# Two-layer convolution block: sampling weights laid out with the eight ky of a cell side by side, layer-norm sums moved from GpSimd to VectorE, and a kernel table built from 16 steps

## The chip, the core and the metric

The kernel runs on one core of a Trainium2 chip. The metric is the device time of one execution in microseconds (us). Three runs of the kernel before took 12570.41, 12572.89 and 12574.23 us, so the median is 12572.89 us. The profile below is of a further execution.

Engine names in the profile: PE is TensorE's matmul, PEld its weight load, DVE is VectorE, ACT ScalarE, POOL GpSimd, SP the engine that issues most DMAs.

## What is computed

The input `x` is 32 images of 128 channels, 32 by 32 pixels, all in float32. Two layers follow, each added to its input after a group norm.

```python
# layer 0: a state-space convolution along the 1024 positions, a gate, a layer norm
h  = einsum('bdl,de->ble', u, W_enc) + b_enc            # 128 -> 1024
K  = 2 * einsum('dn,dnl->dl', Cc * Bd, exp(dtA * t)).real   # t = 0..63
y  = gelu(causal_conv(h, K) + D * h)
g  = y @ W_glu; g = g[..., :1024] * sigmoid(g[..., 1024:])
out = layernorm(h + g) @ W_dec + b_dec
# layer 1: a depthwise 8x8 convolution whose 64 taps sample at learned places
off = depthwise_conv3x3(x)                              # dx, dy of each tap and pixel
for tap in 64:                                          # bilinear sample, times a weight
    acc += bilinear(x, px + off_x, py + off_y) * weight[tap]
out = gelu(batchnorm(acc))
```

## The kernel before

There are three stages. `ssm_kernel_table` (lines 42 to 159) builds K for all 1024 channels: it evaluates exp and sine/cosine at 32 (channel group, mode) pairs times 64 steps, so its VectorE operations have 2048 elements per partition.

`ssm_convolution` (186 to 371) runs over eight groups of 128 channels. `encode(k)` projects the 32 images (line 237) and VectorE copies the sums out of PSUM (L242). Only for k = 0 it also makes the group norm of each image, in five steps that a hand-written loop (264 to 284) puts out for three images in turn: a row sum on ACT (L169), a matmul over groups (L172), the mean and the squares on ACT (L174, L175), a second matmul (L178), and root, reciprocal and scaling (L180 to L182). The normalised image is stored to memory as `u_d` by a DMA that ACT's queue issues (L267). `convolve` then multiplies by a table of K (L320).

`main_block` (590 to 1348) is the long stage. It interleaves two streams of work by `run_along` (577), which always lets the stream with the smaller share of its planned cost speak next. The order of instructions on every engine is therefore fixed when the program is built, and no measured time enters it.

- The first stream is the rest of layer 0, on tiles of 512 positions, two for each image and eight output chunks m for each tile. A chunk has eight matmuls for the gate (L815), eight for the value (L838), one for h (L854), one to decode (L743). ACT takes the sigmoid (L822), VectorE makes the product (L846) and `r = h + g` (L867), ACT squares r (L875). Layer norm needs the sum over chunks of r and of its square: `add_up` (735 to 739) adds them up on GpSimd in two halves of 256, called at L745 for r and at L876 for the square.
- The second stream is layer 1 of an image some way behind. An image has 17 packs, each of m = 8 to 16 slots (12 packs have 16); a slot is one pairing of a source column with a tap column. Per slot the tile `ds` holds 160 cells, eight tap rows ky times 20 rows v, as weights over 128 partitions: two sides of 64 partitions, of eight window columns times eight window rows. ACT makes hat functions of the distance in y in the tile `dhy` (L1153, L1154), and VectorE multiplies `ds`, the hats in x that a DMA brings from memory, by them (L1159, in four parts for a pack). TensorE multiplies by the image's windows `dxw` (L1235). A pack has four pieces, and a piece has a PSUM bank for each side; four banks are there (`psam`, line 627), so a piece can start when the piece two before it has been read out. VectorE does that, scaling with the tap weights into `prod` (L1251), and GpSimd sums over ky (L1278) and adds up to the image (L1286).

Pieces 1 to 3 are each a block of eight ky by four v in two matmuls of two v each. Piece 0 has five small blocks: 2 ky by 6 v, 2 by 4, 2 by 2, 3 by 1 and 4 by 1. Every float32 matmul in the code is two matmul records in the profile, and the two sides run as neighbours on different halves of the array. Before the change a slot's cells lie as 20 v for each ky, so a matmul of pieces 1 to 3 reads its moving operand as runs of two neighbouring floats:

```python
to = t[:, lo:hi].rearrange("p (s k v) -> p s k v", s=m, k=rows)
...
ap=[frm.ap[0], [CELLS, m], [step * NV + skew, rows], [1, r1 - r0]]
```

Between the packs an image is prepared (889 to 1077) in small steps at fixed places of the pack before: group norm, nine taps of the offset convolution on VectorE (L943, L947), the transposition of the offsets (L964, L975), layout DMAs, and eight hats in x on ACT (L1017, L1018), each followed by a store on ACT's queue. There are 12 such places in a pack, and the taps stand three apart.

Of the kernel before, what the change touches and what calls it, by code (L numbers as in the profile page):

```python
# [8 lines left out]
F32 = mybir.dt.float32  # L9
AF = mybir.ActivationFunctionType  # L10
# [31 lines left out]
def ssm_kernel_table(nc, tc, ins, kp_d):  # L42

    KN = KD * N2
    with tc.tile_pool(name="ssm", bufs=1) as sp:
# [88 lines left out]

        big = (P, KN, NT)
        e, ang = small("e", big), small("ang", big)
        t_b = tt[:, None, :].to_broadcast([P, KN, NT])

        def over_t(a):
            return a[:, :, None].to_broadcast([P, KN, NT])  # L140

        nc.vector.tensor_mul(e, over_t(re), t_b)
        nc.scalar.activation(e, e, AF.Exp)
        nc.vector.tensor_mul(ang, over_t(im), t_b)
        sv, cv = sincos(ang, big, "v")
        nc.vector.scalar_tensor_tensor(cv, cv, 1.0, over_t(cbr), op0=ALU.add, op1=ALU.mult)
        nc.vector.tensor_mul(sv, sv, over_t(cbi))
        nc.vector.tensor_sub(cv, cv, sv)
        nc.vector.tensor_mul(cv, cv, e)

# [35 lines left out]
def ssm_convolution(nc, tc, const, ins, x, u_d, kp_d, y_d):  # L186
# [12 lines left out]
    with tc.tile_pool(name="cvt", bufs=3) as tp, tc.tile_pool(  # L199
# [24 lines left out]
        def encode(k):  # L224
# [6 lines left out]

            def image(b, u):
                both = banks(f"psz_{k}_{b}").rearrange("p g (j d) -> p g j d", j=NB)
                for g in range(2):
                    for j in range(NB):
                        lo = block(g, j) * P
                        nc.tensor.matmul(  # L237
                            both[:, g, j, :], u[:, lo : lo + P], w_enc[:, k * P : (k + 1) * P],
                            start=True, stop=True,
                        )  # L240
                for g in range(2):
                    nc.vector.tensor_add(  # L242
                        z[g][:, :, :, b, :].rearrange("p d j e -> p j d e"),
                        both[:, g].rearrange("p j (d e) -> p j d e", e=2),
                        bias.rearrange("p (d e) -> p d e", e=2)[:, None].to_broadcast(
                            [P, NB, P // 2, 2]
                        ),
                    )
# [15 lines left out]
            for t in range(B + 3):  # L264
                step(t - 2)
                if t - 2 in running:
                    nc.scalar.dma_start(u_d[t - 2], running[t - 2][0])  # L267
                step(t - 1)
# [12 lines left out]
                if t >= 3:  # L281
                    image(t - 3, running.pop(t - 3)[0])
                step(t - 1)
                step(t)
# [250 lines left out]
BOUND_X, BOUND_Y = 2.45, 2.45  # L535
HSUB = NCOL // P

# [52 lines left out]
def main_block(nc, tc, const, ins, x, u_d, y_d, x1_d, out, offmax):  # L590
# [22 lines left out]
    with ctx:  # L613
# [121 lines left out]
        def add_up(to, more):  # L735

            for lo in (0, T // 2):
                cut = slice(lo, lo + T // 2)
                nc.gpsimd.tensor_add(to[:, cut], to[:, cut], more[:, cut])  # L739

# [150 lines left out]
        def prepare(b):  # L891
# [112 lines left out]
            def gather():  # L1004
                t = st["t"] = one.tile([P, HSUB], F32, tag="rel", name=f"dr_{b}")
                nc.sync.dma_start(
                    t, at(rel_d[b % 2], 0, [[HSUB, P // 2], [SIDE, 2], [1, HSUB]])
                )

            def hat(k):  # L1010


                def run():
                    if k == 0:
                        st["h"] = dram.tile([2, 8, SIDE], F32, tag="hat_d", name=f"dhat_{b}")
                    t = hatpool.tile([P, HSUB], F32, tag="hat", name=f"dh_{b}_{k}")
                    nc.scalar.activation(t, st["t"], AF.Abs, bias=minus[:, k : k + 1])  # L1017
                    nc.scalar.activation(t, t, AF.Relu, scale=-1.0, bias=const["one"])  # L1018
                    nc.scalar.dma_start(
                        at(  # L1020
                            st["h"], k * SIDE,
                            [[HSUB, P // 2], [8 * SIDE, 2], [1, HSUB]],
                        ),
                        t,
                    )

                return run
# [128 lines left out]
        def weights(h, part):  # L1156

            cut, t = cut_of(h, part)
            nc.vector.tensor_mul(s_of[h][:, cut], s_of[h][:, cut], t)  # L1159
            if part % 2:  # L1160
# [18 lines left out]
        def second_part(b, steps):  # L1179
# [6 lines left out]
            for n in range(NP):  # L1186
# [9 lines left out]
                for i in range(0, PIECES, 2):  # L1196
# [10 lines left out]
                    for piece in (i, i + 1):  # L1207
# [7 lines left out]
                        for parts in zip(blocks_of(0, piece), blocks_of(1, piece)):  # L1215
                            rows, run = parts[0][0][1], parts[0][0][3]
                            hi = lo + rows * run * m
                            to = [
                                t[:, lo:hi].rearrange("p (s k v) -> p s k v", s=m, k=rows)
                                for t in ps  # L1220
                            ]
                            for part in range(len(parts[0][1])):
                                for side in range(2):
                                    (ky, _, v0, _, step, skew), wins = parts[side]
                                    w, r0, r1 = wins[part]
                                    half = slice(64 * side, 64 * side + 64)
                                    frm = s[half, 0, ky * NV + v0 - VBASE[side] + r0 :]
                                    frm = bass.AP(
                                        tensor=frm.tensor, offset=frm.offset,
                                        ap=[  # L1230
                                            frm.ap[0], [CELLS, m],
                                            [step * NV + skew, rows], [1, r1 - r0],
                                        ],
                                    )
                                    nc.tensor.matmul(  # L1235
                                        to[side][:, :, :, r0:r1],
                                        xw[half, w, :], frm, start=True, stop=True,
# [6 lines left out]
                    def scale(piece, side):  # L1244
                        for p, sd, frm, (ky, rows, v0, run, step, skew) in work:
                            if (p, sd) != (piece, side):
# [11 lines left out]
                                ),  # L1258
                                frm,
                                wt[:, :, :, None].to_broadcast([P, m, rows, run]),  # L1260
# [233 lines left out]
```

## Time and profile before

The profiled execution took 12590.62 us, of which its first-to-last-instruction span is 12588.9 us; it is 0.14% above the median of the runs.

| stretch of the span, us | what | PE busy | DVE | ACT | POOL | PE clock |
|---|---|---|---|---|---|---|
| 0 to 48 | kernel table, first images | 11.35 | 37.74 | 23.39 | 6.39 | 1.00 |
| 48 to 188 | rest of encode(0) | 105.97 | 68.98 | 78.43 | 0.00 | 0.78 |
| 400 to 1200 | convolution | 781.81 | 464.34 | 290.65 | 388.11 | 1.00 |
| 1330 to 1640 | first tiles of the main block | 310.00 | 42.30 | 37.67 | 45.90 | 1.00 |
| 1800 to 12230 | both streams | 10309.00 | 6627.81 | 4764.54 | 7823.19 | 1.00 |
| 12230 to 12589 | second stream alone | 175.56 | 216.80 | 141.37 | 290.88 | 0.61 |

Each busy figure is in us within the stretch. An engine whose busy time nearly fills a stretch has no more to give there; the others wait for it or for each other. The clock is the share of TensorE's full speed that was granted. In groups of instructions, "busy" is the union of the times of all of that kind, so that matmuls that overlap count once; "mean" is the length of one record, which for a matmul is longer than its share, since matmuls are pipelined.

### The profile page before, as it was taken

What the parts mean: (1) busy time and instruction counts of PE and PEld (TensorE: products, weight loads), DVE (VectorE), ACT (ScalarE), POOL (GpSimd) and SP (SyncE); (2) the same over time, 40 slices, a digit from 0 to 9 for tenths busy, and PEclk for the clock granted to TensorE, in tenths of its full rate; (3) what the DMA queues carried; (4) which work ended last, traced back from release to release, by engine and by line L of the source; (5) the groups of instructions that cost most, each with busy time, mean ns of one, the idle gap of its engine ahead of it and who ended that gap; (6) DMA issues with size and microseconds to landing.
All of it is one profiled execution on the core that took longest, in us unless ns stands there. A gap on an engine that the chain in (4) does not pass through costs nothing.

```text
span 12588.9 us, 161534 instructions
## 1 busy us (share of the span) xinstructions
PE 12115.7 (96%) x51362; PEld 6608.0 (52%) x51362; DVE 7661.0 (61%) x14315; ACT 5537.8 (44%) x7852; POOL 8789.7 (70%) x11691
## 2 busy tenths in 40 slices
PE   7999889999999999999999999999999999999975
PEld 7999444444444444444444444444444444444443
DVE  5555136666666666666666666666666666666666
ACT  4344124444444444444444444444444444444444
POOL 2455227777777777777777777777777777777778
PEclk9999999999999999999999999999999999999986
DMA  7899236766666666666666666666667667666666
GB/s 236 267 276 277 83 98 185 187 184 184 180 183 180 185 178 182 186 184 181 188 184 187 184 180 185 179 187 180 179 187 186 180 186 186 186 185 184 183 176 177
DMA packets 1521947, 2350.43 MB, mean 187 GB/s; under 512 B 619586, under 2 KB 835266, under 8 KB 1520066
## 3 DMA queue, kind: packets, MB, share of 16 engines
q1 hardware_dynamic: 1382210, 2027.97, 60.1%
q10 hardware_dynamic: 89728, 177.76, 4.2%
q0 software_dynamic: 49152, 134.28, 3.6%
q8 instruction: 414, 6.78, 0.2%
q14 instruction: 443, 3.63, 0.1%
HBM read 2016.61 MB, written 407.02 MB: 193 GB/s over the span
## 4 chain that ended last, share of the span: by engine, by line
PE 77%; DMA 10%; ACT 5%; DVE 3%; issue 2%; SPq 2%; POOL 1%; ACTq 0%; DVEq 0%; POOLq 0%
PE gpv L838 24%; PE gpg L815 23%; PE dps L1235 15%; DMA dhat<-dh 5%; PE psy L320 5%; PE psz L237 3%; PE gpo L743 3%; PE gph L854 3%; DMA rel_d<-rel_n 1%; ACT dh L1018 1%; ACT dh L1017 1%; ACT dhy L1153 1%; POOL prod L1278 1%; DVE ds L1159 1%; DMA dr<-rel_d 1%
## 5 line engine op out<-in xcount | busy, mean ns | idle before, releaser
L1278 POOL TENSOR_TENSOR prod<-prod 128x256 f32<-128x256 f32 (+3 forms) x7616 | 5531.4, 767 | 1211.5 <-DVE prod L1251 1211.5
L1251 DVE TENSOR_TENSOR prod<-dps,k_weight_slots 128x512 f32<-128x512 f32 (+16 forms) x8704 | 3127.5, 407 | 1948.0 <-PE dps L1235 1743.5
L815 PE MATMUL gpg<-gy,g_w_glu 128*128 128x512 f32 x8192 | 3741.9, 600 | 14.3 <-DMA gy<-y_d 14.3
L838 PE MATMUL gpv<-gy,g_w_glu 128*128 128x512 f32 x8192 | 3732.1, 599 | 0.0
L1235 PE MATMUL dps<-ds,dxw 64*128 64x128 f32 (+14 forms) x23936 | 2700.2, 371 | 235.4 <-DVE prod L1251 171.5
L1159 DVE TENSOR_TENSOR ds<-ds,dhy 128x640 f32<-128x640 f32 (+2 forms) x2176 | 2260.0, 1075 | 929.0 <-ACT dhy L1154 673.3
L1235 PEld LDWEIGHTS dps<-ds,dxw 64*128 64x128 f32 x23936 | 1924.2, 194 | 1287.3 <-issue 480.6
L815 PEld LDWEIGHTS gpg<-gy,g_w_glu 128*128 128x128 f32 x8192 | 1511.2, 190 | 1926.2 <-issue 1862.1
L838 PEld LDWEIGHTS gpv<-gy,g_w_glu 128*128 128x128 f32 x8192 | 1514.6, 190 | 1909.2 <-issue 1909.2
L739 POOL TENSOR_TENSOR gs<-gs,gq 128x256 f32<-128x256 f32 x896 | 865.7, 987 | 1820.8 <-ACT gq L875 1820.8
L1153 ACT ACTIVATE dhy<-dhy,k_minus_y 128x640 f32<-128x640 f32 (+2 forms) x2176 | 1697.8, 780 | 384.2 <-DMA dhy<-rel_d 138.1
L1154 ACT ACTIVATE dhy<-dhy,one 128x640 f32<-128x640 f32 (+2 forms) x2176 | 1725.8, 793 | 71.2
L875 ACT ACTIVATE gq<-gr 128x512 f32<-128x512 f32 x448 | 282.3, 630 | 2793.1 <-DVE gr L867 2775.9
L822 ACT ACTIVATE gs<-gpg,k_b_glu 128x512 f32<-128x512 f32 x512 | 350.8, 685 | 1657.0 <-PE gpg L815 1655.7
L357 POOL DMA_DIRECT2D y_d<-yo x1024 | 591.5, 585 | 692.2 <-ACT yo L344 634.1
L846 DVE SCALAR_TENSOR_TENSOR gs<-gpv,k_b_glu,gs 128x512 f32<-128x512 f32 x512 | 382.9, 748 | 1008.6 <-PE gpv L838 983.2
L1286 POOL TENSOR_TENSOR dacc<-dacc,prod 128x256 f32<-128x256 f32 (+6 forms) x1184 | 862.8, 729 | 55.2
L739 POOL TENSOR_TENSOR gs<-gs,gr 128x256 f32<-128x256 f32 x896 | 798.0, 911 | 0.0
L320 PE MATMUL psy<-toe,z 128*128 128x192 f32 x4096 | 668.3, 326 | 7.6 <-DVE z L242 5.5
L320 PEld LDWEIGHTS psy<-toe,z 128*128 128x128 f32 x4096 | 663.4, 196 | 11.7 <-DVE z L242 6.8
L854 PE MATMUL gph<-gu,k_W_enc 128*128 128x512 f32 x1024 | 529.2, 598 | 27.7 <-DVE gs L846 27.4
L335 DVE TENSOR_TENSOR psy<-psy,t 128x256 f32<-128x256 f32 (+2 forms) x768 | 333.8, 435 | 346.3 <-ACT t L328 329.5
(164 smaller groups left out, 6020.0 us busy)
## 6 DMA issues: line engine op xcount, KB each, us to landing
dhy<-rel_d SPq DMA_DIRECT2D x3264, 160.0 KB
ds<-dhat SPq DMA_DIRECT2D x832, 400.0 KB
ds<-dhat SPq DMA_DIRECT2D x448, 480.0 KB
dxw<-dxw_d SPq DMA_DIRECT2D x832, 224.0 KB
y_d<-yo POOLq DMA_DIRECT2D x1024, 128.0 KB, 4.2
gy<-y_d SPq DMA_DIRECT2D x512, 256.0 KB
u<-u_d SPq DMA_DIRECT2D x224, 512.0 KB
dhat<-dh ACTq DMA_DIRECT2D x256, 390.0 KB
```

The source lines that it names most:

```text
L320: nc.tensor.matmul(ps[:, c // 2, c % 2, :], rows[i][:, (g * CG + c0 + c) // 2, c % 2, :], toe[:, c0 + c, :], start=True, stop=True,)
L739: nc.gpsimd.tensor_add(to[:, cut], to[:, cut], more[:, cut])
L815: nc.tensor.matmul(gate, w_glu[:, k, D + m * P : D + m * P + P], ys[k], start=(k == 0), stop=(k == KD - 1),)
L838: nc.tensor.matmul(val, w_glu[:, k, m * P : m * P + P], ys[k], start=(k == 0), stop=(k == KD - 1),)
L854: nc.tensor.matmul(h, w_enc[:, m * P : (m + 1) * P], u, start=True, stop=True)
L1153: nc.scalar.activation(t, t, AF.Abs, bias=minus_y)
L1154: nc.scalar.activation(t, t, AF.Relu, scale=-1.0, bias=const["one"])
L1159: nc.vector.tensor_mul(s_of[h][:, cut], s_of[h][:, cut], t)
L1235: nc.tensor.matmul(to[side][:, :, :, r0:r1], xw[half, w, :], frm, start=True, stop=True,)
L1251: nc.vector.tensor_mul(bass.AP(tensor=at_y.tensor, offset=at_y.offset, ap=[at_y.ap[0], [H, m], [step * (KS - 1) + skew, rows], [1, run],], ...
L1278: nc.gpsimd.tensor_add(row(to, lo, hi), row(to, lo, hi), row(frm, lo, hi))
L1286: nc.gpsimd.tensor_add(to, to, total[:, slot * H : (slot + nj) * H].rearrange("p (s y) -> p s y", y=H),)
```

## The change

Three parts.

1. A slot's cells lie as eight ky for each v. ACT writes the x hats in that order (it reads its input across), the hat tile has 104 partitions of 960 elements in place of 128 of 780, and the moving operand and the PSUM tile are indexed (slot, v, ky). VectorE's L1159 reads `dhy` across, and L1251 reads PSUM across, to keep its write as it was.
2. `add_up` is one VectorE addition of 512 elements in place of two GpSimd additions of 256.
3. The kernel table is evaluated at 16 steps (56, 48, ..., 0 and 7, 6, ..., 0), and each of the 64 values comes from a product of one of the first eight and one of the last eight, real and imaginary parts apart. In encode(0), the store of `u_d` is issued by GpSimd's queue, and one group-norm step is placed between the two halves of an image's projection.

```diff
-        big = (P, KN, NT)
-        e, ang = small("e", big), small("ang", big)
+        few = (P, KN, 16)
+        nc.vector.tensor_copy(t16[:, 0:8], tt[:, 7::8])
+        nc.vector.tensor_copy(t16[:, 8:16], tt[:, NT - 8 : NT])
...
+        sv, cv = sincos(ang, few, "v")
+        nc.vector.scalar_tensor_tensor(cv, cv, 1.0, e, op0=ALU.add, op1=ALU.mult)
+        nc.vector.tensor_mul(sv, sv, e)
...
+        nc.vector.tensor_mul(w[0], near[0], over_t(cbr, 8))
+        nc.vector.tensor_mul(w[2], near[1], over_t(cbi, 8))
+        nc.vector.tensor_sub(w[0], w[0], w[2])
+        nc.vector.tensor_mul(w[1], near[0], over_t(cbi, 8))
+        nc.vector.tensor_mul(w[2], near[1], over_t(cbr, 8))
+        nc.vector.tensor_add(w[1], w[1], w[2])
+        for i, far in enumerate((cv, sv)):
+            o = small(f"o{i}", (P, KN, 8, 8))
+            nc.vector.tensor_mul(
+                o,
+                w[i][:, :, None, :].to_broadcast([P, KN, 8, 8]),
+                far[:, :, :8, None].to_broadcast([P, KN, 8, 8]),
+            )
...
+        nc.vector.tensor_sub(cv, cv, parts[1])
...
-            def image(b, u):
+            def image(b, u, between=None):
...
+                    if g == 0 and between is not None:
+                        between()
...
-                    nc.scalar.dma_start(u_d[t - 2], running[t - 2][0])
+                    nc.gpsimd.dma_start(u_d[t - 2], running[t - 2][0])
...
-                    image(t - 3, running.pop(t - 3)[0])
-                step(t - 1)
+                    image(t - 3, running.pop(t - 3)[0], between=lambda: step(t - 1))
+                else:
+                    step(t - 1)
...
-HSUB = NCOL // P
+ROWS = 104
+HSUB = NCOL // ROWS
...
         def add_up(to, more):
-
-            for lo in (0, T // 2):
-                cut = slice(lo, lo + T // 2)
-                nc.gpsimd.tensor_add(to[:, cut], to[:, cut], more[:, cut])
+            nc.vector.tensor_add(to, to, more)
...
-                    nc.scalar.activation(t, st["t"], AF.Abs, bias=minus[:, k : k + 1])
+                    nc.scalar.activation(
+                        t.rearrange("p (s v k) -> p s v k", v=NV, k=8),
+                        st["t"][:ROWS].rearrange("p (s k v) -> p s v k", v=NV, k=8),
+                        AF.Abs, bias=minus[:ROWS, k : k + 1],
+                    )
...
-            nc.vector.tensor_mul(s_of[h][:, cut], s_of[h][:, cut], t)
+            x = s_of[h][:, cut].rearrange("p s (v k) -> p s v k", k=8)
+            nc.vector.tensor_mul(x, x, t.rearrange("p s (k v) -> p s v k", k=8))
...
-                                t[:, lo:hi].rearrange("p (s k v) -> p s k v", s=m, k=rows)
+                                t[:, lo:hi].rearrange("p (s v k) -> p s v k", s=m, k=rows)
...
-                                    frm = s[half, 0, ky * NV + v0 - VBASE[side] + r0 :]
+                                    frm = s[half, 0, (v0 - VBASE[side] + r0) * 8 + ky :]
...
-                                            [step * NV + skew, rows], [1, r1 - r0],
+                                            [8, r1 - r0], [step + 8 * skew, rows],
...
-                                        to[side][:, :, :, r0:r1],
+                                        to[side][:, :, r0:r1, :],
...
-                                frm,
+                                frm.rearrange("p s v k -> p s k v"),
```

A matmul of pieces 1 to 3 now reads runs of 16 neighbouring floats (two v of eight ky). In piece 0 the first three blocks read runs of two where they read runs of six, four and two; the block of 4 ky by 1 v reads runs of four where it read single floats; the block of 3 by 1 reads single floats as before.

## Prediction

> **What bounds the kernel now.** I read the page first: its engine shares, then its slices.
>
> ```profile
> PE 12115.7 (96%) x51362; PEld 6608.0 (52%) x51362; DVE 7661.0 (61%) x14315; ACT 5537.8 (44%) x7852; POOL 8789.7 (70%) x11691
> ...
> PE   7999889999999999999999999999999999999975
> ```
>
> PE is the only engine near full, and from the seventh slice to the last but two it is at nine tenths or more. Next, the busy times by stretch.
>
> ```profile
> 48.00:188.00 140.00, 105.97 (x627) 99.47 (x628) 68.98 (x125) 78.43 (x179) 0.00 (x0) 0.78 0.61 212
> 1800.00:12230.00 10430.00, 10309.00 (x41036) 5099.70 (x41035) 6627.81 (x12347) 4764.54 (x6328) 7823.19 (x10187) 1.00 0.68 183
> 12230.00:12589.00 359.00, 175.56 (x947) 135.95 (x944) 216.80 (x443) 141.37 (x180) 290.88 (x377) 0.61 0.67 175
> ```
>
> Columns are length, then busy PE, PEld, DVE, ACT, POOL, then clock. In the long stretch PE idles 121 us of 10430 (DVE is at 64%, POOL 75%), so a shorter matmul is a shorter kernel, as long as DVE keeps up. From one image's L964 to the next's it is 341 us for 17 packs, 20.06 us a pack.
>
> Then PE's order of time, for the spacing of matmuls.
>
> ```profile
> 6015.98 3.60 PE L815 MATMUL gpg<-gy,g_w_glu 128*128 128x512 f32 x8
> ...
> 6019.86 1.50 PE L1235 MATMUL dps<-ds,dxw 64*128 64x256 f32 x10
> ...
> 6009.36 0.44 PE L1235 MATMUL dps<-ds,dxw 64*128 64x192 f32 x4
> ...
> 6009.53 0.39 PE L1235 MATMUL dps<-ds,dxw 64*128 64x128 f32 x4
> ...
> 6010.13 0.43 PE L1235 MATMUL dps<-ds,dxw 64*128 64x64 f32 x4
> ...
> 6010.27 0.58 PE L1235 MATMUL dps<-ds,dxw 64*128 64x64 f32 x4
> ```
>
> A stretch of n equal matmuls lasts n-1 spacings and one record. L815: (3.60 - 0.59)/7 = 0.43 us for 512 columns, 0.838 ns a column, reading contiguously. L1235's ten are five pairs of sides (the two of a pair start 9 ns apart): (1.50 - 0.43)/4 = 0.267 us for 256 columns, 1.043 ns a column, reading runs of two. The 64x192 pair, runs of six, is followed by the next pair after 9.53 - 9.36, in the record 0.162: 0.84 ns a column, full rate. Two 64-column pairs that read single floats stand 0.14 apart: 2.18 ns a column, while their PSUM writes are contiguous. So the slow rate follows the read: 2.09 ns for each new group of neighbours. Small pairs never go below 0.112 (two weight loads).
>
> **Part 1, PE.** Runs of 16 should go at 0.838. In the records, pairs of 256, 224, 208 and 128 columns with runs of two stand 267, 233, 217 and 133 ns apart; at full rate 214.5, 188, 174 and the floor of 112. The groups by shape give the numbers of records; four records make two pairs.
>
> ```profile
> L1235 PE MATMUL dps<-ds,dxw 64*128 64x256 f32 x9216 | 1455.7, 446 | 2.0 <-DVE prod L1251 2.0
> ```
>
> 4608 pairs x 52.5 ns = 242 us; 768 x 45 = 35; 768 x 43 = 33; 384 x 21 = 8. Sum 318. Piece 0 pays: its 192-column pair goes to runs of two, 162 to 200 ns, 768 pairs, 29 us, with the smaller packs 37; the 128-column pair from 112 to 133, 768 pairs, with the smaller 17; the 4-by-1 pair gains, 140 to 112 on 768, with the smaller 30. Net -24. If the rate followed the write instead, the first two losses would be nil. So 294, between 280 and 318 (and 0, if the rival about runs holds). The tail's 947 records, 44 to a pack, are 22 of the 544 packs, where PE waits anyway; the other 522 save **282 us**, 0.54 a pack.
>
> Here the rule of the Trainium skill is to be weighed. "SBUF — State Buffer", Specifications (TRN2), says that two hits on a 16-byte line give full bandwidth. By it, runs of two floats cost nothing and part 1 gains nothing. The rows say 2.5 against 2 units a column, and I take the rows.
>
> **Part 1, DVE.** Its rows:
>
> ```profile
> L1159 DVE TENSOR_TENSOR ds<-ds,dhy 128x640 f32<-128x640 f32 x1728 | 1860.0, 1111 | 654.1 <-ACT dhy L1154 427.0 <-DMA ds<-dhat 173.2 <-DMA dxw<-dxw_d 33.3
> L1251 DVE TENSOR_TENSOR prod<-dps,k_weight_slots 128x512 f32<-128x512 f32 x2304 | 1578.5, 685 | 129.1 <-PE dps L1235 28.6 <-DVE prod L1251 1.8
> ...
> L964 DVE SCALAR_TENSOR_TENSOR drel<-dco,k_base_x 128x1024 f32<-128x1024 f32 x32 | 68.3, 2134 | 0.0
> ...
> L784 DVE TENSOR_TENSOR gd<-gd,grs 128x512 f32<-128x512 f32 x64 | 49.3, 770 | 2.2
> ...
> L975 DVE TENSOR_TENSOR drel<-drel,k_base_y 128x1024 f32<-128x1024 f32 x32 | 48.4, 1513 | 0.0
> ```
>
> No row shows DVE reading single floats across. The nearest is L964, which writes them 128 bytes apart: (2134 - 1513)/1024 = 0.61 ns an element above L975; L1251's blocks of single floats show 0.72 above its blocks of pairs (260 against 214 ns for 64 elements). I take 0.68. The same page's rule, a penalty for each line that is hit once, speaks against the change here too: L1159 reads every float of `dhy` 80 bytes from the last. Bounds: 0, if only writes suffer, and 1.05 (PE's 2.09 less DVE's own 1.04). L1159 handles 1.30 M elements per partition: 885 us of DVE (0 to 1370).
>
> L1251 reads PSUM 32 bytes apart: 1.56 M elements in pieces 1 to 3 and 0.39 M in the blocks of two ky. No row shows such a read. I take 0, since the nearest rows (L964, the single-float blocks) are of SBUF; the other end is 0.68, 1330 us. It is the second rival. A gain is excluded for both: they are contiguous now.
>
> ACT's hats grow from 780 to 960 elements. From L1153's 480 (683) and 640 (815) 0.825 ns an element: +0.15 us x 512 = 76 us, at most +160 for reading across, on an engine at 46%, hidden. If that cover went, only the tail would see it.
>
> **Part 2.** GpSimd loses L739's 1664 us and goes from 75% to about 61%. It sets no end, so that gains nothing but shorter blocking of DVE. DVE gets 896 additions of 512; L784 has that form at 770 ns: 690 us. At L876 DVE waits for ACT's square (L875, 630 ns); ACT is already waiting there 420 times of 448, so the wait is about 0.65 us x 448 = 290 us. Queued behind it are L1251's reads, on which the next piece's matmuls wait.
>
> DVE in the long stretch: 6628 + 690 + 849 (L1159's part of it) = 8167 of 10430 - 282 = 10148, 80%, with the waits 83%. PE stays the bound on average, but not in every pack. The preparation's DVE work (8 taps at 1.36 and the rest, 17.4 us an image) falls into three packs. A pack has 6628/520 = 12.75 us of DVE on the mean (10430/20.06 = 520 packs), such a pack 12.75 - 1.02 + 5.8 = 17.5; the change adds 1.3 (additions), 0.6 (waits) and 1.6 (L1159), which makes 21.0 against 20.06 - 0.54 = 19.5 of PE. Three packs lack 4.5 us an image; about 1 us of it I take as absorbed, since two PSUM pieces can queue: 3.5 us x 31 images, **+110 us** (0 to 250).
>
> **Part 3.** The table's 13 DVE operations of 2048 elements (ten at 2.29, three at 1.22, 26.6 us) become ten of 512 (0.68 and less, 6 us), seven small (2 us), three of 2048 (6.9): -12 us, on the path, since images 0 to 2 wait behind them until 48 us. Then 29 images take 140 us, 4.8 each, while ACT itself needs 3.0 (its rows L169 to L180). ACT's store issue waits for DVE's L182 (1.47 us idle at L174) and takes 0.35. Moved to POOL's queue, which is idle there (0.00), and with the group matmul no longer behind eight projections, 3.9 is fair: -25 us (0 to -40; 0.5 MB in and 0.5 MB out at 3.4 us an image are 308 GB/s, and the most that a slice of the page shows is 277). Together **-37**.
>
> **Tail.** 359 us, the second stream alone. Some 20 L1159 lie on its chain, +0.44 each, and 16 hat operations +0.15: **+12**. The planner's costs are unchanged, so the order of the streams is.
>
> **Sum** on the profiled execution: 12590.6 - 282 + 110 - 37 + 12 = 12394; the runs' median is 18 lower: **12376 us**, 1.5% faster. Its own range is 12250 to 12520.
>
> **Rivals.**
> - *Reads across cost DVE nothing* (chance 0.18). L1159 stays at 1111, the three packs need 19.4, the stall is some 10 us: 12276. For it: no read in the trace is slow on DVE. Against: PE's reads are.
> - *DVE becomes the bound through PSUM* (0.30). L1251 at 685 + 0.68 x 512 = 1030 ns puts 2.4 us on each pack: the three packs need 23.4, lack 11.7 less the 1, some 330 us over 31 images, and an ordinary pack, at 17.7 of 19.5 us, loses an estimated 0.4 us, 170 more over 430. 12590.6 - 282 - 37 + 12 + 500 - 18 = 12766, slower. It turns from gain to loss when stalls pass 307 us, that is from about 0.34 ns an element on L1251's reads. For it: "PSUM — Partial Sum Buffer" of the skill gives PSUM lines of two floats and says that other than contiguous access slows matmuls, so each such read is a new line; no run here shows that for DVE. Against: PE writes a column there each 0.84 ns, a faster pace than DVE's reads.
> - *Longer runs don't speed PE up* (0.06), the 1.04 being of the shape and not of the read: 12376 + 282 = 12658. Against: the 192-column pair.
> - The remaining 0.04: gains and stalls cancel.
>
> **Chances.** A measurement can tell 0.2%, 25 us, from no change. First case 0.42 and the free reads 0.18 give faster 0.60; same 0.06; slower 0.34. The range 12250 to 12800 leaves out the upper half of the PSUM case and a few hundredths below.
>
> **What would show it.** L1235's ten 256-column records in 1.29 us instead of 1.50; the 192-column pair at 0.20. L1159 at about 1.5 us for 640, L1251 at 0.69. PE's idle in the long stretch at some 230 us, put down to L1251, most in the packs with L947. The first table step under 40 us and encode(0) done by 151. The forecast is wrong if L1251 is above 0.85, or PE's idle above 430.

## The result, and the profile after

The changed kernel is slower: 13144.71 us (median of 4 runs, 13143.44 to 13157.94) against 12571.65 us for the kernel before on the same chip, a ratio of 1.0454 (95% interval 1.0442 to 1.0467), or +573 us. The profiled execution took 13157.94 us with a span of 13156.1. The forecast was 12376 us, which is faster than before: its sign was wrong, and the time lies outside its range.

The page's engine shares and TensorE's slices, after:

```profile
PE 12195.4 (93%) x51362; PEld 6724.6 (51%) x51362; DVE 8887.7 (68%) x15220; ACT 5835.1 (44%) x7851; POOL 7922.1 (60%) x9931
...
PE   8998979999999999999999999999999999999974
```

TensorE's share has fallen from 96% to 93%: outside its busy time lie 961 us instead of 473. The busy time itself has *grown* by 80 us, although the long matmuls of the second stream have become faster. The stretches show both (length, busy PE, PEld, DVE, ACT, POOL, then the granted clock):

```profile
48.00:188.00 140.00, 123.33 (x883) 117.43 (x882) 86.41 (x171) 102.14 (x234) 55.08 (x98) 1.00 0.90 285
1800.00:12230.00 10430.00, 9912.63 (x39018) 4973.72 (x39017) 7379.73 (x12512) 4799.42 (x6006) 6611.59 (x8044) 0.97 0.67 174
12230.00:12800.00 570.00, 487.49 (x1973) 262.57 (x1971) 417.67 (x691) 245.35 (x314) 381.47 (x458) 0.86 0.68 172
12800.00:13156.00 356.00, 161.01 (x882) 128.23 (x882) 239.79 (x412) 144.42 (x175) 295.63 (x345) 0.60 0.61 165
```

In the long stretch TensorE now idles 517 us of 10430 (121 before), the stretch goes on for 570 us more, and the clock column has dropped from 1.00 to 0.97 and 0.86. The tail, where the second stream runs alone, has grown too: from TensorE's last decoding matmul (L743 before, L764 after) to the end it is 505 us, where it was 468. VectorE, which the prediction watched, is at 71% there, not at the 80 to 83% it computed. From one image's L985 to the next's it takes 359 us, where L964 to L964 took 341.

**The single operations.** First TensorE's order of time, one line of the kernel before and one of the changed kernel:

```profile
6019.50 2.40 PE L1235 MATMUL dps<-ds,dxw 64*128 64x256 f32 x16
```

```profile
6024.16 2.00 PE L1262 MATMUL dps<-ds,dxw 64*128 64x256 f32 x16
```

Then the groups by shape (count, then busy us, mean ns, idle before), on VectorE after the change, and on ScalarE before and after:

```profile
L1186 DVE TENSOR_TENSOR ds<-ds,dhy 128x640 f32<-128x640 f32 x1728 | 2294.8, 1373 | 693.3 <-ACT dhy L1180 336.8 <-DMA ds<-dhat 315.3 <-DMA gy<-y_d 34.2
L1278 DVE TENSOR_TENSOR prod<-dps,k_weight_slots 128x512 f32<-128x512 f32 x2304 | 1583.8, 687 | 84.1 <-DVE prod L1278 0.9
L760 DVE TENSOR_TENSOR gs<-gs,gq 128x512 f32<-128x512 f32 x448 | 431.1, 962 | 386.4 <-ACT gq L896 386.4
...
L760 DVE TENSOR_TENSOR gs<-gs,gr 128x512 f32<-128x512 f32 x448 | 371.2, 829 | 0.0
```

```profile
L1018 ACT ACTIVATE dh<-dh,one 128x780 f32<-128x780 f32 x256 | 242.0, 945 | 8.3
L1017 ACT ACTIVATE dh<-dr,k_minus 128x780 f32<-128x780 f32 x256 | 240.9, 941 | 407.4 <-DMA dhat<-dh 368.9 <-DMA dr<-rel_d 38.5
```

```profile
L1039 ACT ACTIVATE dh<-dr,k_minus 104x960 f32<-104x960 f32 x256 | 500.4, 1955 | 678.6 <-DMA dhat<-dh 492.2 <-DMA dr<-rel_d 186.2
...
L1044 ACT ACTIVATE dh<-dh,one 104x960 f32<-104x960 f32 x256 | 280.4, 1095 | 8.3
```

Sixteen 256-column records take 2.00 us where the kernel before needs 2.40. They are eight pairs with seven spacings: (2.40 - 2.00)/7 is 57 ns a pair, and 52.5 was forecast. L1278, which now reads PSUM across, is at 687 ns against 685: that read costs nothing. L1186 has gone from 1111 to 1373. The surprise is L1039, ScalarE's first hat step: 1955 ns, where L1017 before took 941 and where L1044, of the same length but read straight, takes 1095. Reading across costs ScalarE 0.86 us, or 0.90 ns an element.

**Where TensorE waits**, from 1830 to 12200 us in both kernels (total us, times, longest). Before:

```profile
PE dtr L1038 <- DVE prod L1251: 43.2, 32, 7.0
PE gph L854 <- DVE gs L846: 27.4, 25, 3.1
PE dps L1235 <- DVE prod L1251: 20.2, 21, 3.6
```

After:

```profile
PE dps L1262 <- DVE prod L1278: 159.3, 107, 4.2
PE dtr L1064 <- DVE prod L1278: 155.9, 29, 5.8
PE gph L875 <- DVE gs L867: 96.6, 29, 5.4
PE gpg L836 <- DMA gy<-y_d: 74.4, 29, 3.8
```

Counted by place, 337 us of the 517 lie two to six packs behind L985, which are the packs with the hats and the two behind them (a good 40 before), and 151 in the pack with the transpositions `dtr` (41 before), one of those in which the prediction expected DVE to fall behind.

The row for `gy`, which has no counterpart before, comes through another queue: SP issues these loads in order with those of the second stream, and ahead of 24 of the 27 such waits over 0.3 us its queue had stood, for more than 2.5 us, until the store of a hat had landed.

One stall in a hat pack shows the chain. TensorE, then VectorE, then ScalarE (start us, length; in brackets the idle time before it and what ended it):

```profile
6028.77 1.02 PE L789 MATMUL gpq<-gs,davg 128*128 128x512 f32 x2
6035.18 1.22 PE L875 MATMUL gph<-gu,k_W_enc 128*128 128x512 f32 x1 [5.39 <-DVE gs L867]
```

```profile
6029.70 0.99 DVE L1186 TENSOR_TENSOR ds<-ds,dhy 128x480 f32<-128x480 f32 x1 [8.67 <-ACT dhy L1180]
...
6034.35 0.77 DVE L867 SCALAR_TENSOR_TENSOR gs<-gpv,k_b_glu,gs 128x512 f32<-128x512 f32 x1
```

```profile
6024.28 1.96 ACT L1039 ACTIVATE dh<-dr,k_minus 104x960 f32<-104x960 f32 x1 [4.56 <-DMA dhat<-dh]
6026.27 1.09 ACT L1044 ACTIVATE dh<-dh,one 104x960 f32<-104x960 f32 x1
6027.39 0.81 ACTq L1045 DMA_DIRECT2D dhat<-dh  x1
6028.25 0.69 ACT L1179 ACTIVATE dhy<-dhy,k_minus_y 128x480 f32<-128x480 f32 x1 [0.89 <-ACT dh L1044]
6028.97 0.69 ACT L1180 ACTIVATE dhy<-dhy,one 128x480 f32<-128x480 f32 x1
```

Read from below: ScalarE waits 4.56 us for the store of the previous hat (the hats have one buffer), then spends 3.86 us on one hat and its store, and only then comes to the `dhy` that VectorE has been waiting for. VectorE stands 8.67 us, works off its products, and comes to `gs` L867 at 6034.35. That is the only thing TensorE needs, and it was queued behind all of it. This is no single case: of the 29 waits of over 1 us for this `gs` from 1830 to 12200 us, 28 have a wait for `dhy` as VectorE's longest in the 15 us before.

**The clock after a stall.** The first matmul after this stall lasts 1.22 us, twice its usual 0.59. The ten microseconds from 6034 on:

```profile
6034.00:6044.00 10.00, 8.82 (x20) 3.67 (x22) 5.02 (x8) 6.39 (x7) 4.29 (x7) 0.66 0.73 210
```

The clock records show 6.8 us at half speed from 6034.1, then full speed again. From 1830 to 12200 us there are 121 such windows, 118 of them of 3.4 or 6.8 us and three of 10.2, 693 us together; before, in the same stretch, there were 7 (102 us). In that stretch of after, so many of TensorE's gaps longer than 0.3 us had such a window in the 5 us behind them: 21 of 75 gaps under 1 us, 29 of 51 from 1 to 2, 19 of 24 from 2 to 3, and 74 of 75 above 3. A short gap that lies near a longer one is counted here with it: only 2 of the 121 windows have no gap of 1 us in the 8 us before them, but 48 have none above 3 us. The Trainium skill ("TensorE: Matmul & The Clock Gate", Part 1: The HAM clock gate) says that the clock falls to half after an idle window of about 3.4 us; the trace agrees for the long gaps, and shows that shorter ones are enough at times. Length alone does not decide it: in the kernel before, 3 of 45 gaps of 1 to 2 us had such a window behind them. The prediction, which counted idle time alone, did not have this.

So the account of the profiled execution's +567 us is: +488 us outside PE's busy time, and +80 in it. By the clock records the part of PE's busy time that ran at half speed grew from 292 to 866 us in the whole span; half of the difference, 287 us, is what the clock cost. The faster matmuls took back the rest: 80 = 287 - 207. The run with TensorE's part alone (e9, below) shows 270 us for them; where the other 60 or so went is open.

### The profile page after: what moved, and what is told of

Same layout as the page of the kernel before. It is cut to its first block, busy times and chain, and to the rows that moved or that the text cites. A ratio compares the mean times of both kernels' runs of the same rounds, so it can differ in the third digit from the quotient of the medians.

```text
span 13156.1 us, 161162 instructions
## 1 busy us (share of the span) xinstructions
PE 12195.4 (93%) x51362; PEld 6724.6 (51%) x51362; DVE 8887.7 (68%) x15220; ACT 5835.1 (44%) x7851; POOL 7922.1 (60%) x9931
## 4 chain that ended last, share of the span: by engine, by line
PE 56%; DMA 16%; ACT 11%; DVE 7%; issue 4%; SPq 4%; POOL 1%; ACTq 1%; DVEq 0%; POOLq 0%
PE gpg L836 18%; PE gpv L859 16%; PE dps L1262 10%; DMA dhat<-dh 9%; PE psy L343 5%; ACT dh L1039 4%; DVE ds L1186 3%; PE psz L257 3%; DMA rel_d<-rel_n 3%; ACT dh L1044 2%; PE gpo L764 2%; ACT dhy L1179 2%; PE gph L875 2%; DVE prod L1278 2%; DMA ds<-dhat 2%
## 5 line engine op out<-in xcount | busy, mean ns | idle before, releaser
L1305 POOL TENSOR_TENSOR prod<-prod 128x256 f32<-128x256 f32 (+3 forms) x7616 | 6065.2, 834 | 4528.8 <-DVE prod L1278 4528.7
L836 PE MATMUL gpg<-gy,g_w_glu 128*128 128x512 f32 x8192 | 3957.9, 628 | 110.1 <-DMA gy<-y_d 90.8
L1278 DVE TENSOR_TENSOR prod<-dps,k_weight_slots 128x512 f32<-128x512 f32 (+16 forms) x8704 | 3134.2, 407 | 1052.1 <-PE dps L1262 812.5
L1186 DVE TENSOR_TENSOR ds<-ds,dhy 128x640 f32<-128x640 f32 (+2 forms) x2176 | 2784.1, 1326 | 1050.8 <-ACT dhy L1180 606.2
L1262 PE MATMUL dps<-ds,dxw 64*128 64x128 f32 (+14 forms) x23936 | 2545.9, 351 | 451.1 <-DVE prod L1278 352.5
L1262 PEld LDWEIGHTS dps<-ds,dxw 64*128 64x128 f32 x23936 | 1978.4, 196 | 1403.4 <-issue 709.6
L836 PEld LDWEIGHTS gpg<-gy,g_w_glu 128*128 128x128 f32 x8192 | 1577.8, 199 | 2119.0 <-issue 1898.0
L1313 POOL TENSOR_TENSOR dacc<-dacc,prod 128x256 f32<-128x256 f32 (+6 forms) x1184 | 1052.1, 889 | 55.2
L867 DVE SCALAR_TENSOR_TENSOR gs<-gpv,k_b_glu,gs 128x512 f32<-128x512 f32 x512 | 382.7, 747 | 745.9 <-PE gpv L859 719.0
L1039 ACT ACTIVATE dh<-dr,k_minus 104x960 f32<-104x960 f32 x256 | 500.4, 1955 | 678.6 <-DMA dhat<-dh 492.2
L760 DVE TENSOR_TENSOR gs<-gs,gq 128x512 f32<-128x512 f32 x448 | 431.1, 962 | 386.4 <-ACT gq L896 386.4
```

What stands on the lines that cost most here:

```text
L836: nc.tensor.matmul(gate, w_glu[:, k, D + m * P : D + m * P + P], ys[k], start=(k == 0), stop=(k == KD - 1),)
L1039: nc.scalar.activation(t.rearrange("p (s v k) -> p s v k", v=NV, k=8), st["t"][:ROWS].rearrange("p (s k v) -> p s v k", v=NV, k=8), AF.Abs ...
L1186: nc.vector.tensor_mul(x, x, t.rearrange("p s (k v) -> p s v k", k=8))
L1262: nc.tensor.matmul(to[side][:, :, r0:r1, :], xw[half, w, :], frm, start=True, stop=True,)
L1278: nc.vector.tensor_mul(bass.AP(tensor=at_y.tensor, offset=at_y.offset, ap=[at_y.ap[0], [H, m], [step * (KS - 1) + skew, rows], [1, run],], ...
L1305: nc.gpsimd.tensor_add(row(to, lo, hi), row(to, lo, hi), row(frm, lo, hi))
```

## Experiments

Three theories stood at first. **A**: ScalarE's hat steps make the stalls. **B**: the sums on VectorE do, through its wait in order for ScalarE's square. **C**: VectorE's mere load does. Each ratio is to the kernel before on the same chip; since that took 12572 to 12647 us on the chips used, ratios are compared, and 1% is 126 us.

**e1: sums back on GpSimd.**

```diff
-            nc.vector.tensor_add(to, to, more)
+            for lo in (0, T // 2):
+                cut = slice(lo, lo + T // 2)
+                nc.gpsimd.tensor_add(to[:, cut], to[:, cut], more[:, cut])
```

> The changed kernel, with the layer-norm sums put back on GpSimd in two halves; all else as changed. Three theories, against 12572 us before and 13145 after. A (hat steps): ACT's x-hat step, 1.95 + 1.10 us with its read across and a longer store, holds up the hats in y, the squares and the sigmoids behind it in ACT's order; TensorE's stalls then also cost clock. The sums only pass it on: 12950 to 13050. B (sums): VectorE's in-order wait for ACT's square (386 us at L760, up to 12.8 at once) is what brings ACT's lateness to the PSUM read-out: it goes, and with it most of the loss, 12450 to 12650. C (VectorE's load): 802 us less on VectorE takes away the stall in the packs with taps, 158 us of idle and some 135 of half clock: about 12880, with the stalls in the packs with hats left.

12966.58 us, ratio 1.0305 (1.0288 to 1.0322), which is in A's range. The sums' move costs 1.49%, 187 us: real, but a third of the loss. B as the only cause is out.

**e2: the hats read straight** (the cells then come in the wrong order), and **e3: also as 128 x 780.**

```diff
-                        t.rearrange("p (s v k) -> p s v k", v=NV, k=8),
-                        st["t"][:ROWS].rearrange("p (s k v) -> p s v k", v=NV, k=8),
-                        AF.Abs, bias=minus[:ROWS, k : k + 1],
+                        t, st["t"][:ROWS], AF.Abs, bias=minus[:ROWS, k : k + 1]
```

```diff
-ROWS = 104
+ROWS = 128
```

> The changed kernel, with ACT's first hat operation reading its input straight instead of across (104 partitions by 960 as changed); the cells of a slot then stand in the wrong order, so that part of the computation is left out, with the same instructions and sizes otherwise. L1039 should fall from 1955 to about 1095 ns. A: the idle of the packs with hats (350 us) and most of their half-clock time go: 12550 to 12700. B: a square is late less often, but VectorE still waits for each: 12850 to 13000. C: no more than 100 us: 13050.

> As the one with straight hats, and the hat tile as before: 128 partitions by 780, so that a store goes over 16 DMA engines and not 13 (the order of the cells is wrong here too). A with the store as a part of it: 50 to 100 us less than the straight one. A without: within 20 us of it. B and C: as for the straight one.

e2: 12898.67 us, 1.0251 (1.0234 to 1.0269); e3: 12725.81 us, 1.0117 (1.0100 to 1.0134). Reading across in the hats costs 2.03% (255 us), the narrow form another 1.34% (168 us), more than A gave it. Together they are the largest part, 423 us. A's number for e2 was nevertheless missed by 200 us, and e2 lies in the range that B gave. No single theory holds; the parts seem to add.

**e4: the layout off** (the kernel before with the sums on VectorE and with part 3), and **e5: part 3 alone.**

> The kernel before with the sums on VectorE and the short kernel table, without the new layout. A: the sums alone do little, since ACT's hat steps are short: 12550 to 12600. B: the waits for the square alone hold up PSUM: 12750 or more. C: VectorE has 800 us more and no reads across: 12600 to 12700, stalls in the packs with taps.

> The kernel before with part 3 alone (table from steps 8a + b, the encoder's order at the start); correct. All theories: the start is off the main stage, so the time falls by what the first 150 us lose, 30 to 45 us: 12530 to 12550 against some 12575. If the 19 us that the start seemed to give in the changed kernel is all of it: 12555.

e4: 12661.97 us, 1.0063 (1.0046 to 1.0079); e5: 12550.05 us, 0.9960 (0.9946 to 0.9974). Part 3 gains some 50 us. The sums on VectorE cost 1.03%, 129 us, even with the old layout (e4 lies in C's range).

**e6: the layout with straight, wide hats and the sums on GpSimd**, and **e9: the same with the weights' product straight too.**

```diff
-            x = s_of[h][:, cut].rearrange("p s (v k) -> p s v k", k=8)
-            nc.vector.tensor_mul(x, x, t.rearrange("p s (k v) -> p s v k", k=8))
+            x = s_of[h][:, cut]
+            nc.vector.tensor_mul(x, x, t)
```

> The changed kernel with the sums on GpSimd and the hats straight and 128 x 780, so that the cells come in the wrong order (the output is not the reference's): of the layout, only the matmuls' longer runs and the reading across at the weights' product on VectorE are left. Theory A (ScalarE's hat steps and their store make the stalls): the three parts add, 13145 - 419 - 178 = 12550 at most, and since each part alone still left stalls from the other, 12400 to 12550. Theory C (VectorE's load makes them): the product read across is still 640 columns at 1.3 us, so stalls stay: 12500 to 12600. The next run tells the two apart.

> The run before it with the weights' product read straight as well (wrong order of the cells, output not the reference's): only TensorE's longer runs and part 3 are left. If TensorE's saving of 282 us is simply the time saved where nothing else has changed: 12575 - 282 - 37 = 12255, between 12240 and 12300. If a faster TensorE runs into VectorE and waits more: 12350 to 12450. Theory C also wants a difference of over 150 us to the run before it; theory A under 60.

e6: 12566.36 us, 0.9975 (0.9966 to 0.9985); e9: 12361.01 us, 0.9811 (0.9795 to 0.9828). So reading the product across on VectorE costs 1.64%, 206 us, which is theory C's difference and not A's. And TensorE's longer runs, with VectorE's free read of PSUM across and everything else as before, are worth 1.49% over e5, 187 us, in the range of the second expectation. The pages tell why that is not the full saving; e5, then e9:

```profile
PE 12093.9 (96%) x51362; PEld 6587.8 (53%) x51362; DVE 7659.3 (61%) x14324; ACT 5534.8 (44%) x7851; POOL 8795.9 (70%) x11723
```

```profile
PE 11823.9 (96%) x51362; PEld 6564.1 (53%) x51362; DVE 7738.4 (63%) x14324; ACT 5534.3 (45%) x7851; POOL 8796.7 (71%) x11723
```

PE's busy time falls by 270 us (the part of it at half speed is the same, 249 and 254 us), and 86 us come back as idle time.

From these runs the whole change can be walked in six steps, each with one part more. In another order the figures can differ (the sums, taken out of the changed kernel first, gave 187):

| step | part | ratios | us |
|---|---|---|---|
| before to e5 | table and encoder | 1 to 0.9960 | -50 |
| e5 to e9 | TensorE's longer runs | 0.9960 to 0.9811 | -187 |
| e9 to e6 | weights' product across on VectorE | 0.9811 to 0.9975 | +206 |
| e6 to e3 | sums on VectorE | 0.9975 to 1.0117 | +179 |
| e3 to e2 | hats as 104 x 960 | 1.0117 to 1.0251 | +168 |
| e2 to changed | hats across on ScalarE | 1.0251 to 1.0454 | +255 |

The sum is 571 us by construction; each step is uncertain by some 30 us.

**e13, e12, e11: one part alone on the kernel before with part 3.** Do these costs need a faster TensorE that has used up the slack?

```diff
-            nc.vector.tensor_mul(s_of[h][:, cut], s_of[h][:, cut], t)
+            x = s_of[h][:, cut].rearrange("p s (v k) -> p s v k", k=8)
+            nc.vector.tensor_mul(x, x, t.rearrange("p s (k v) -> p s v k", k=8))
```

> The kernel before with part 3, and the weights' product on VectorE reading and writing across as in the changed kernel (so it pairs wrong cells: the output is not the reference's). In the changed kernel reading it straight gave back 205 us. If the parts simply add: 12550 + 205 = 12755. If VectorE has slack for it while TensorE is slower: 12550 to 12620.

```diff
-HSUB = NCOL // P
+ROWS = 104
+HSUB = NCOL // ROWS
...
-                    nc.scalar.activation(t, st["t"], AF.Abs, bias=minus[:, k : k + 1])
+                    t = t[:ROWS]
+                    nc.scalar.activation(
+                        t, st["t"][:ROWS], AF.Abs, bias=minus[:ROWS, k : k + 1]
+                    )
```

> Correct: the kernel before with part 3, and the hats as 104 partitions of 960, still read straight. In the changed kernel, with straight hats, going from 104 x 960 to 128 x 780 gave back 173 us. If the parts simply add: 12550 + 173 = 12720. If the price of the narrow form is slack that only a faster TensorE has used up: 12550 to 12620.

```diff
             if m > 0:
                 add_up(sums[0], r)
+                add_up(sums[1], sq)
...
-                        add_up(sums[1], sq)
-                        pending["decode"] = (m, r, sums, dec)
+                        pending["decode"] = (m, r, sums, dec, sq)
```

> Correct: the kernel before with part 3 and the sums on VectorE, in which the square is added one column block later, behind the other sum, so that VectorE no longer waits for ScalarE's square; VectorE's work is the same as with the sums in their changed place (which took 12662, against 12550 with part 3 alone). If the wait in order makes the 112 us: 12545 to 12580. If VectorE's added 690 to 800 us of work makes them: 12630 to 12670.

e13: 12718.83 us, 1.0091 (1.0074 to 1.0107), 1.31% over e5, 165 us. e12: 12736.21 us, 1.0110 (1.0093 to 1.0127), 1.50%, 189 us. Neither needs the faster TensorE: there was no slack to begin with. No run has the hats read across alone. e11: 12618.02 us, 1.0013 (1.0004 to 1.0021), 67 us over e5, where e4 was 129 over. VectorE's wait for the square has gone, and half of the cost has gone with it. The additions of the square in e4, then in e11:

```profile
L759 DVE TENSOR_TENSOR gs<-gs,gq 128x512 f32<-128x512 f32 x448 | 375.7, 839 | 350.2 <-ACT gq L895 350.2
```

```profile
L759 DVE TENSOR_TENSOR gs<-gs,gq 128x512 f32<-128x512 f32 x448 | 412.7, 921 | 7.9 <-ACT gq L896 7.7
```

Whether the other half is VectorE's load or the new order is open: TensorE's waits at `dtr` are back at e5's 44 us (85 in e4), but those for `gs` have grown to 86 (29 in e4). The measured time lies between the two expectations.

In e13, with the sums on GpSimd as before, the product is at 1536 ns against e5's 1099:

```profile
L1182 DVE TENSOR_TENSOR ds<-ds,dhy 128x640 f32<-128x640 f32 x1728 | 1840.0, 1099 | 673.4 <-ACT dhy L1177 423.1 <-DMA ds<-dhat 189.4 <-DMA dxw<-dxw_d 43.5
```

```profile
L1183 DVE TENSOR_TENSOR ds<-ds,dhy 128x640 f32<-128x640 f32 x1728 | 2579.4, 1536 | 470.1 <-ACT dhy L1177 247.5 <-DMA ds<-dhat 177.9 <-DMA dxw<-dxw_d 28.3
```

That is 0.68 ns an element, the size taken in the prediction; in the changed kernel the mean is lower, but so is that of the straight product once the sums have left GpSimd (939 ns in e4), and (1373 - 939)/640 is 0.68 ns again. The effect runs the other way too: GpSimd's additions over ky take 855 ns in e13 against 790 in e5, and its busy time rises from 8796 to 9572 us with the same work. TensorE's waits show both ends of it: at `dtr`, for VectorE, they go from 44 to 89 us, and for the sums on GpSimd from 5 to 38 us. How the 165 us divide between the two engines is open.

**e14: ScalarE's extra time without the narrow store.** Why should 104 x 960 cost 189 us? Per hat it adds 0.30 us in the two steps (1094 and 1096 against 941 and 945) and 0.28 in the store's issue (0.81 against 0.53), about 150 us of ScalarE in all. Here the steps work on 960 columns of 128 partitions, a copy of 64 columns (244 ns) stands for the issue, and 780 columns are stored.

```diff
+HLONG = 960
...
+                    nc.scalar.copy(t[:, HSUB : HSUB + 64], t[:, HSUB + 64 : HSUB + 128])
...
-                        t,
+                        t[:, :HSUB],
```

> Correct: the kernel before with part 3 and the hats stored as 128 x 780, but each hat takes about as much of ScalarE as the 104 x 960 form with its longer issue (columns 780 to 960 are worked on and not stored, and a third step copies 64 of them). If it is the time on ScalarE that made the narrow form 186 us slower: 12700 to 12740. If it is the store and its landing on fewer DMA engines: 12550 to 12600.

12649.65 us, 1.0002 (0.9994 to 1.0011): 53 us over e5, give or take 20, and between the two expectations. They were set against a chip on which the kernel before takes 48 us less; with that taken off, e14 is at the edge of the second. So ScalarE's time is about 30% of the narrow form's price, and the rest must come with the store. It is 104 packets of 3840 bytes where before it is 128 of 3120, and its landing is told by 13 semaphore updates, with one more right at the issue, where before there are 16; this speaks for 13 DMA engines in place of 16. From the start of the issue to the last byte it takes 4.43 us in e12 and 3.30 in e14 (medians); 0.28 of the difference is the longer issue, for which e14's copy stands. That the later landing is the rest is argued; no run changes the landing alone. TensorE's longest-waiting row in e12 fits: `gph` for VectorE's `gs`,

```profile
PE gph L878 <- DVE gs L870: 107.0, 30, 5.1
```

30 times, once an image, where e14 has 31.3 us and e5 29.7. Ahead of 29 of these 30, VectorE's longest wait in 15 us was for hats on their way back from memory (`ds`<-`dhat`).

**e8, e10, e15: turning the order once an image.** Instead of reading across eight times in ScalarE's hats and in each product, GpSimd turns the distances of x and y once (1.84 us each), they go back to memory, and hats (128 x 780) and products read straight; the sums are on GpSimd. The cells come in the right order. e8 does it in the steps that are free; e10 uses more buffers; e15 also starts the hats later.

```diff
-                (150, gather), *((154 + 4 * k, hat(k)) for k in range(8)),
+                (149, take(0)), (154, turned(0)), (155, put(0)),
+                (157, take(1)), (160, gather), (161, turned(1)), (162, put(1)),
+                *((164 + 3 * k, hat(k)) for k in range(8)),
```

> Correct: the distances are turned once an image by GpSimd and sent through DRAM in the order that TensorE wants, for x and for y; the hats are then 128 x 780 and straight, the weights' product is straight, the sums are on GpSimd. Theory A: the stalls go and TensorE's saving stays: 12260 to 12400, below both kernels. Rival: GpSimd's in-order wait for two gathers of about 4 us each and two turns of 2 us or more holds up the sums of the feed-forward part, about 12 us an image: 12450 to 12600.

> Correct: as the run that turns both distances once an image, with the steps spread out: the raw and the turned pieces lie in tiles that are free at that time, the second gather is asked for well after its data has gone out, and the hats have two buffers. If that run's stalls were those of its schedule alone (ScalarE waiting for the second gather, SyncE's queue held behind it): 12350 to 12450, below both kernels. If the turn itself is what costs (about 1.8 us of GpSimd twice an image, 6.8 us for each store from its queue): 12500 to 12700.

> Correct: both distances turned once an image, with the hats' start moved behind the second gather's landing (in the run before, ScalarE waited up to 15 us for it, 30 times) and the second take and the second gather asked for only when their data is there. If those waits were the rest of the loss: 12380 to 12500, below both kernels. If the hats' tighter spacing (every three steps, not four) and SyncE's queue cost as much: 12550 to 12700.

e8: 13057.81 us, 1.0361 (1.0343 to 1.0378), outside both expectations. e10: 12667.30, 1.0054 (1.0037 to 1.0071), and e15: 12602.84, 0.9963 (0.9951 to 0.9976), each in the range of its second one. In all three the turned distances arrive after ScalarE has come to the first hat in its order; in e15 still:

```profile
ACT dh L1071 <- DMA dr<-rel_t: 362.6, 30, 14.3
```

ScalarE stands 12 us an image at its first hat, and what is queued behind that hat stands too. e15 beats the kernel before by 0.37%, no more than e5 with part 3 alone (0.40%). How much of e9's 1.9% can be had in the right order stays open.

## Why the prediction was wrong, point by point

- **The bound.** "A shorter matmul is a shorter kernel, as long as DVE keeps up" was right about TensorE and wrong in its condition. DVE at 71% keeps up on the mean, and TensorE still waits, since VectorE waits in order for ScalarE, and ScalarE in order for a store.
- **Part 1, PE: right.** 282 us forecast; e9 against e5 shows 270, with equal work at half speed in both. The rows were the better guide than the rule weighed there. Of it 187 reach the end, since 86 us come back as idle time.
- **Part 1, DVE: sizes right.** L1278 (L1251 before) stayed at its time, and reading SBUF across costs 0.68 ns an element, the size that the prediction took from writes. But its price is more than a share of a stall in three packs: alone it costs 165 us (e13), with the faster TensorE 206 (e6 against e9), and it slows GpSimd, which the prediction left out.
- **Part 1, ACT: the step that failed.** The prediction wrote: "ACT's hats grow from 780 to 960 elements ... +0.15 us x 512 = 76 us, at most +160 for reading across, on an engine at 46%, hidden. If that cover went, only the tail would see it." The time itself was put too low: 371 us (79 for the length, 220 for reading across, and 72 for the store's longer issue, which was not counted) instead of at most 236. "Hidden" was wrong: the two halves of this change cost 168 + 255 = 423 us of the 571. The hats fall into three packs of an image, one buffer ties each to the landing of the last store, and `dhy` and with it VectorE's products and `gs` are queued behind them. A mean of 46% says nothing of these packs. Of the 769 us between forecast and measurement, by the six steps, 411 are the hats (423, less the 12 for the tail), 275 VectorE's product and sums (385 instead of 110) and 95 the part of TensorE's saving that did not reach the end; part 3 gained 13 more than forecast.
- **Part 2: too low.** 690 us of additions were 802 (962 and 829 ns instead of 770), the waits 386 instead of 290. The prediction put no price on them beyond the three packs with taps. They cost 129 us alone, half of it from the wait in order (e11), and 179 to 187 with the layout.
- **The three packs with taps: place right.** Idle time in the `dtr` pack went from 41 to 151 us, and e4 and e13 show that the sums and the product each bring some of it. That the difference is just the 110 forecast is in part luck: the sums took more of VectorE than forecast, the product less (1373 ns, where 1111 and 0.68 x 640 make 1546), and the work at half clock behind each stall was left out.
- **Part 3: right in kind.** -37 forecast, some -50 measured (e5). The first projection starts at 25.9 us (31.2 before), the images follow each other every 3.03 us, where the prediction took 3.9, and PE begins the convolution at 131.5 us (181.3 before).
- **The clock: missing.** Each stall of some microseconds was counted at its length. Behind nearly every one above 3 us TensorE ran at half speed, mostly for another 3.4 to 6.8 us; all of it cost some 287 us, beside 488 us of added time outside PE's busy time.
- **The rivals.** "DVE becomes the bound through PSUM" has the sign, but not the mechanism: its test was L1251 (L1278 after) above 0.85 us, and that is 0.687. The other test, PE's idle time above 430 us, fired (517), for a cause that no rival named. The other two rivals are out: reads across cost DVE 0.68 ns an element, and longer runs do speed PE up, by 57 ns a pair. So the chance of 0.34 for "slower" rested, but for 0.04, on a mechanism that did not occur.
- **Tail: too low.** +12 us forecast, +37 measured from the last decoding matmul on.

## What to carry to other kernels

Before calling an added operation hidden, look at what is queued behind it on its own engine in the stretch where it falls, and at who waits for that; an engine's mean share does not answer it. In a stretch where the main engine is at 99% through tight hand-offs, each added wait is paid on its own: here a part that was run alone cost most of what it cost beside others (165 and 206 us, 189 and 168, 129 and 179). And price a stall of the matmul engine at its length plus the work that follows at half clock.

## What the runs showed of the hardware that was not expected

- TensorE's clock goes to half, mostly for 3.4 or 6.8 us, after stalls: in the changed kernel behind 74 of 75 gaps above 3 us and 29 of 51 of 1 to 2 us, before behind 3 of 45 of the latter.
- Reading SBUF 80 bytes apart costs ScalarE 0.90 ns an element (1955 against 1095 ns for 960) and VectorE 0.68 (1536 against 1099 ns for 640); VectorE's read of PSUM 32 bytes apart costs nothing (687 against 685 ns for 512).
- A store of the same bytes takes longer from 104 partitions (13 updates tell of its landing) than from 128 (16): its issue takes 0.81 us instead of 0.53, and from the start of the issue to the last byte it is 4.25 us in the changed kernel and 3.90 before (medians), most of which is the issue.
- VectorE's product is slower with GpSimd's sums beside it: read across it takes 1538 ns with them (e1) and 1373 without, read straight 1099 (e5) and 939 (e4). The product read across slows GpSimd in turn: its additions over ky take 855 ns instead of 790 (e13, e5).
